# Walk products through three banks, row sums read out with their product, no transfers issued by GpSimd: a two-layer graph kernel on one core

## The chip, the core and the metric

The kernel runs on one core of a Trainium2 chip. The metric is the time of one execution in microseconds of device time. The kernel before took 1558.84 us, the median of three runs (1557.53 to 1560.49). Engines are named as the profile names them: PE is the matmul engine (TensorE), ACT is ScalarE, DVE is VectorE, POOL is GpSimd, and SP is the engine that only issues transfers.

## The reference

There are N = 2708 nodes with 256 features each, and a sparse adjacency matrix of N x N. Layer 0 does two steps, and each has a walk and an attention:

```python
R = S + jnp.eye(N); R = R / R.sum(-1, keepdims=True)     # S is adj
Xf, Xa, Z = X, X, 0
for n in range(2):
    A = top_p_attention(Xa, W1, W2, W3)   # softmax(q k^T), the largest entries up to a mass of 0.9, renormalised
    Xf = R @ Xf                            # the walk
    Xa = A @ Xa                            # the attention
    Z = Z + Xf @ U1[n].T + Xa @ U2[n].T
x = layernorm(X + layernorm(X + Z))
```

Layer 1 is a graph attention with four heads over the mask adj != 0 (with the diagonal set), a residual and a layer norm.

## The kernel before

**Tiles.** The nodes lie in 22 row tiles: 16 of 128 rows and 6 of 110, in 11 pairs (PAIRS). All data is fp32.

**The order of the work.** Each engine runs its instructions in the order in which the program issues them; only SP's transfers are put in order by the framework. The program hands out work in slots. `slot(spend)` advances the searches that are under way (`going`), then everything in `doing`, then one piece of the mixing, and then takes `spend` matmuls from the generator `walks()` (`stream`). A `yield` in one of these generators is thus a place where other work comes between.

**Attention.** For each tile, `search` makes the scores (L784 on PE, exponentials L788 on ACT), and in step 1 `survey` looks for a threshold: ACT goes over the row four times (`tally`, L809), and POOL works out the next threshold in between (L829 to L841, whose result is `rth`). DVE then cuts (`bound`, L857 to L878), finds maxima (L889), sorts (L902 to L918), and masks the row (L955, L958). `step` turns the masked row block by block (L259 on PE, the copy eT L264 on ACT) and multiplies it (L277 on PE) into the bank `att`, which ACT reads (L1286).

**The walk.** R @ X is done over pairs of tiles by a scheme of seven products in place of eight. `mixes()` builds the sums of adjacency blocks beside the first attention step (POOL, L720) and stores them as S1 to S4, D11 and D22. Each of the seven products of a pair takes one block as the stationary operand (11 pieces, loaded by SP three products ahead into four buffers, L670 and L682) and one operand from the node features or from their sums T1 to T4 (L1000 to L1006). A product is 11 matmul calls (L1086), which the profile counts as 22. Products lie in two banks, `walk0` and `walk1`, by turns. The order is D11, S2, A12, S3, S1, D22, S4 (PHASES). D11 and A12 accumulate in one bank, as do S2 and S3, and S1 and S4. When a product ends it is read out: ACT copies p1 (D11, L1093) and xa (A12, L1097); DVE makes y1 (S2, L1095), y2 (S3, L1099) and the rest of xa and xb (S1 L1101, D22 L1103, S4 L1105). In the first walk, A12 and S1 carry one column more, the row sums; DVE takes their reciprocal `rinv` straight from the bank (L1108).

After the first walk of a tile, `after_walk0` scales and adds on POOL (L1159, L1160) and stores the rows to `xmd` (L1161). Before the second walk the rows are fetched back (`return_rows`) and the sums T1 to T4 are made anew (`reblend`, `blend`); until that is done, the second walk may do only its first product. The second walk's results go to `finish` (ACT L1226, then POOL and norms), which makes the input of layer 1.

**When.** The first attention step runs without the walk. Then, between the steps, 14 walk calls go to a slot (SPEND_BETWEEN) while the first searches of step 1 begin. In step 1 each block of attention is followed by 11 or 12 walk calls (SPEND_1).

**Layer 1.** `neighbours` fetches a row of adjacency (L239) and makes it a mask with Sign and Square on ACT (L240, L241). `weights` makes the weights on DVE (L1566), `values` and `denominators` multiply them on PE (L1578, L1588). The first two masks are fetched and made at the third-last block of the last attention tile (`early`).

**Transfers that POOL issues.** Halves of q to the other partitions (L760), the terms c1, c2, c3 to DRAM (L1206, L1220, L1288), c1 back (`ca`, L1051), and the walk's rows (L1161).

Of the kernel before, what the change touches and what calls it, by code (L numbers as in the profile page):

```python
# [16 lines left out]
P = 128  # L17
# [28 lines left out]
def kernel(  # L46
# [186 lines left out]
    def neighbours(g, j, adjp):  # L233

        k = rows[j]
        i0, i1 = off[spans[g][0]], off[spans[g][-1] + 1]
        bar = adjp.tile([P, NT - HT, P], F32, name="blk")
        bar = bar.rearrange("p t d -> p (t d)")[:k, : i1 - i0]
        nc.sync.dma_start(bar, adjT[off[j] : off[j + 1], i0:i1])  # L239
        nc.scalar.activation(bar, bar, AF.Sign)  # L240
        nc.scalar.activation(bar, bar, AF.Square)  # L241
        if j in spans[g]:
            own = bar[:, off[j] - i0 : off[j + 1] - i0]
            nc.vector.tensor_tensor(own, own, ident[:k, :k], op=ALU.max)
        return bar
# [299 lines left out]
    def fast_layer0(ep, adjp):  # L545
# [196 lines left out]
        def project(s, c0, w, pj, xT, copy_q, copy_k):  # L742

            for lo, hi, h in ((c0, min(c0 + w, HN), 0), (max(c0, HN), c0 + w, 1)):
                if lo >= hi:
                    continue  # L750
                here, there = slice(h * DA, (h + 1) * DA), slice((1 - h) * DA, (2 - h) * DA)
                at = slice(lo - c0, hi - c0)
                for c in range(DC):
                    nc.tensor.matmul(
                        pj[:, at], wkqk[:, c, h : h + 2].rearrange("p h e -> p (h e)"),
                        xT[:, c, at], start=(c == 0), stop=(c == DC - 1),
                    )
                copy_k(kT[s][here, lo - h * HN : hi - h * HN], pj[here, at])
                copy_q(qT[there, lo:hi], pj[there, at])
                nc.gpsimd.dma_start(qT[here, lo:hi], qT[there, lo:hi])  # L760
# [233 lines left out]
        def blend(name, j0, j1, k):  # L994
# [22 lines left out]
        PHASES = (  # L1017
            ("D11", "B11", 0, True), ("S2", "T2", 1, True), ("A12", "B21", 0, False),
            ("S3", "T3", 1, False), ("S1", "T1", 0, True), ("D22", "T4", 1, True),
            ("S4", "B22", 0, False),  # L1020
        )

        def walks():
# [4 lines left out]
            queue = [(s, i, n) for s in range(STEPS) for i in range(PAIRS) for n in range(7)]  # L1028

            def load(s, i, n):  # L1030
                if (s * PAIRS * 7 + i * 7 + n) % 4 == 3:
                    blk = compact(fourth, rows[2 * i])
                else:
                    blk = new_block(rows[2 * i])
                key = PHASES[n][0]
                if key == "A12":
                    fetch(blk, 2 * i, 1)
                else:
                    get(key, i, blk)
                return blk  # L1040

            def beside(s, t):
# [7 lines left out]
                if not s:  # L1050
                    nc.gpsimd.dma_start(ca[:m], c1[t][:m])  # L1051
                    return ca, None
# [10 lines left out]
            blocks = [load(*queue[at]) for at in range(AHEAD)]  # L1063
            walking.append(True)
            yield
            for at, (s, i, n) in enumerate(queue):
                a, b = 2 * i, 2 * i + 1
                m = rows[a]
                _, name, bank, start = PHASES[n]
                while s and (owing & {(t, 0) for t in (NT - 2, NT - 1)} or (n and blending)):  # L1070
                    yield True
                blk = blocks.pop(0)
                if at + AHEAD < len(queue):
                    blocks.append(load(*queue[at + AHEAD]))
                if n == 0:
                    use = {}
                    xa, xb = (rowp.tile([P, D], F32, name="xw", bufs=4) for _ in range(2))
                if start:
                    use[bank] = ps_wk.tile([P, CHUNK], F32, name=f"walk{(bank + i) % 2}")
                if n == (3 if s else 0):  # L1080
                    aside = {t: beside(s, t) for t in (a, b)}
                w = HALF + 1 if s == 0 and n in (0, 2, 4) else HALF
                ac = use[bank][:m, :w]
                for j in range(PAIRS):
# [5 lines left out]
                    if j == PAIRS - 1:  # L1090
                        left = ac[:, :HALF]
                        if n == 0:
                            nc.scalar.copy(p1[:m], left)  # L1093
                        elif n == 1:
                            nc.vector.tensor_add(y1[:m], left, p1[:m])  # L1095
                        elif n == 2:
                            nc.scalar.copy(xa[:m, :HALF], left)  # L1097
                        elif n == 3:
                            nc.vector.tensor_add(y2[:m], left, p1[:m])  # L1099
                        elif n == 4:  # L1100
                            nc.vector.tensor_add(xb[:m, HALF:], left, y2[:m])  # L1101
                        elif n == 5:
                            nc.vector.tensor_add(xb[:m, :HALF], left, y2[:m])  # L1103
                        else:
                            nc.vector.tensor_add(xa[:m, HALF:], left, y1[:m])  # L1105
                        if s == 0 and n in (2, 4):
                            t = a if n == 2 else b
                            nc.vector.reciprocal(rinv[:m, t : t + 1], ac[:, HALF : HALF + 1])  # L1108
                        if (s, i) == (0, PAIRS - 1):
                            if n in (2, 4, 6):  # L1110
                                return_rows(n)
                            for t, xw, h in {
                                2: ((a, xa, 0),), 5: ((b, xb, 0),), 6: ((b, xb, 1), (a, xa, 1))
                            }.get(n, ()):
                                owing.add((t, h))
                                doing.append(last_rows(t, xw[:m], aside[t][0], h))
                                next(doing[-1])
                            if n == 6:
                                blending.append(True)
                                doing.append(reblend())  # L1120
                        else:
                            for t, xw, last in ((b, xb, 5), (a, xa, 6)):
                                if n == last:
                                    doing.append((after_walk0, finish)[s](t, xw[:m], *aside[t]))
                                    next(doing[-1])
                    yield
            walked.append(True)

        def return_rows(n):

            assert len(rows_kept) == NT - 2
            odd, cols = {2: (None, slice(0, HALF)), 4: (0, second), 6: (1, second)}[n]
# [22 lines left out]

        def after_walk0(t, xw, ca, _):
# [4 lines left out]
            nc.gpsimd.dma_start(xmd[:m, t], xw)  # L1161
# [30 lines left out]
        def terms1(t, xT):  # L1192
# [13 lines left out]
            nc.gpsimd.dma_start(c1[t][:m], cs[:m])  # L1206

        def terms2(t, xT):
# [11 lines left out]
            nc.gpsimd.dma_start(c2[t][:m], cs[:m])  # L1220
# [47 lines left out]
        def step(s, cur, spend):  # L1268
            turned_first = None
            for t in range(NT):  # L1270
# [11 lines left out]
                def between(n):  # L1282
                    last = n == len(groups) - 1
                    if last:
                        xa = heldp.tile([P, D], F32, name="xa1")
                        nc.scalar.activation(xa[:m], ac[:m, :D], AF.Copy, scale=rden)  # L1286
                        if s and t in c3:
                            nc.gpsimd.dma_start(c3[t][:m], xa[:m])  # L1288
# [5 lines left out]
                    if s and (t, n) == (NT - 1, len(groups) - 3):  # L1294

                        early.extend(neighbours(0, j, adjp) for j in first[:2])
# [468 lines left out]
```

## Time and profile before

| | |
|---|---|
| median of three runs | 1558.84 us |
| profiled execution | 1558.56 us, of which the span from the first to the last instruction is 1556.7 us |
| PE, mean granted clock | 0.989 |
| attention step 0 | about 70 to 441.9 us |
| between the steps | 441.9 to 524.9 us |
| attention step 1, with the rest of both walks | 524.9 to about 1200 us |
| layer 1 | from about 1200 us |
| transfers issued by POOL (software queue) | 14.58 MB, 2.9% of the DMA engines' span |
| HBM over the span | 162 GB/s |

The page gives the busy time of each engine, the same in 40 slices, the DMA queues, the chain that ended last and the costliest groups of instructions. A group's line has the source line, engine, operation, output and input, the count, the busy time with the mean of one, and the idle time before it with what ended it. The waits list has: who waited, for whom, us in total, how many times, the longest. A timeline line has start, duration, engine, line, operation and operands, and in brackets the idle time before it and what ended it.

### The profile page before, as it was taken

The numbers are of one execution on the slowest core, as the hardware profiler recorded it, in microseconds if no ns is written. First come the engines' busy times: TensorE is split into PE (matmuls) and PEld (weight loads), VectorE is DVE, ScalarE is ACT, GpSimd is POOL, SyncE is SP. The second block draws the span as 40 slices with busy tenths as digits, with TensorE's granted clock in tenths as the row PEclk, the third lists the DMA queues.
The fourth block names the chain that finished last, engine by engine and source line by source line (L and its number), as shares of the span: only waits on it lengthen the run. The fifth ranks groups of instructions, "written<-read, shape, count | busy, mean of one in ns | idle before, by whom it ended". The sixth has DMA issues, their size and how long they took to land. (4 is left out here: it accounts for less than half of the span.)

```text
span 1556.7 us, 29932 instructions
## 1 busy us (share of the span) xinstructions
PE 1496.2 (96%) x10537; PEld 1068.6 (69%) x10537; DVE 1295.4 (83%) x3763; ACT 801.1 (51%) x1472; POOL 642.4 (41%) x1063
## 2 busy tenths in 40 slices
PE   8999999999998899999989999999999999999993
PEld 4477777777787888888978888888887234333442
DVE  4599999999524887888889898989894998999994
ACT  3444444444334555655656666666653444556572
POOL 2267787865034223423443454544433300144142
PEclk9999999999998999999999999999999999999997
DMA  5198988894047555554555555654454365344331
GB/s 159 55 269 262 287 273 261 259 270 143 12 145 219 175 153 169 165 164 133 168 173 155 171 180 174 182 179 145 143 165 152 113 186 158 97 117 119 94 103 32
DMA packets 204210, 255.99 MB, mean 164 GB/s; under 512 B 42201, under 2 KB 166813, under 8 KB 204049
## 3 DMA queue, kind: packets, MB, share of 16 engines
q1 hardware_dynamic: 192224, 234.36, 50.0%
q0 software_dynamic: 5664, 14.58, 2.9%
q10 hardware_dynamic: 6161, 5.03, 1.1%
q8 instruction: 85, 1.39, 0.4%
q14 instruction: 76, 0.62, 0.1%
HBM read 190.10 MB, written 62.44 MB: 162 GB/s over the span
## 5 line engine op out<-in xcount | busy, mean ns | idle before, releaser
L809 ACT ACTIVATE junk<-e,minus,rth 128x2708 bf16<-128x2708 f32 (+1 forms) x88 | 232.9, 2647 | 60.0 <-POOL rth L841 59.2
L264 ACT COPY eT<-tr 128x512 f32<-128x512 f32 (+5 forms) x264 | 141.6, 536 | 214.0 <-PE tr L259 211.1
L277 PE MATMUL att<-xm,eT 128*128 128x256 f32 (+3 forms) x968 | 230.8, 379 | 0.3 <-ACT xa L1286 0.3
L277 PE MATMUL att<-ba,eT 128*128 128x256 f32 (+3 forms) x968 | 230.9, 379 | 0.0
L1578 PE MATMUL acc<-pt,v 128*32 128x512 f32 (+3 forms) x2112 | 221.2, 543 | 3.4 <-DVE pt L1566 2.3
L1566 DVE SCALAR_TENSOR_TENSOR pt<-e,tj,blk 128x1024 f32<-128x1024 f32 (+3 forms) x176 | 184.6, 1113 | 10.7 <-ACT blk L241 7.5
L1086 PE MATMUL walk<-xe,blk 128*128 128x128 f32 (+6 forms) x1452 | 180.8, 275 | 7.0 <-DVE xw L1105 2.4
L277 PEld LDWEIGHTS att<-xm,eT 128*128 128x128 f32 (+3 forms) x968 | 169.6, 186 | 22.0 <-ACT xa L1286 0.7
L277 PEld LDWEIGHTS att<-ba,eT 128*128 128x128 f32 (+3 forms) x968 | 169.5, 186 | 22.0 <-ACT eT L264 0.8
L1086 PEld LDWEIGHTS walk<-xe,blk 128*128 128x128 f32 (+3 forms) x1452 | 172.0, 187 | 17.2 <-issue 7.2
L788 ACT ACTIVATE e<-lg 128x1024 f32<-128x1024 f32 (+1 forms) x132 | 121.1, 922 | 108.5 <-PE lg L784 98.0
L1578 PEld LDWEIGHTS acc<-pt,v 128*32 128x32 f32 (+1 forms) x2112 | 73.3, 110 | 134.0 <-issue 99.5
L259 PE MATMUL tr<-ident,e 128*128 128x128 f32 (+3 forms) x968 | 147.5, 271 | 4.5 <-ACT eT L264 4.5
L1086 PE MATMUL walk<-xm,blk 128*128 128x128 f32 (+3 forms) x1100 | 140.9, 278 | 4.5 <-DVE xm L1002 2.8
L259 PEld LDWEIGHTS tr<-ident,e 128*128 128x128 f32 (+3 forms) x968 | 111.3, 139 | 46.7 <-issue 26.7
L1086 PEld LDWEIGHTS walk<-xm,blk 128*128 128x128 f32 (+3 forms) x1100 | 133.0, 189 | 14.4 <-issue 7.8
L1588 PE MATMUL acc<-pt,sb 128*32 128x512 f32 (+3 forms) x1056 | 114.8, 542 | 0.0
L1566 DVE SCALAR_TENSOR_TENSOR pt<-r,tj,blk 128x1024 f32<-128x1024 f32 (+1 forms) x88 | 109.8, 1311 | 1.3 <-issue 0.6
L240 ACT ACTIVATE blk<-blk 128x1024 f32<-128x1024 f32 (+3 forms) x66 | 63.3, 961 | 81.6 <-DMA blk<-in_adjT_dram 73.6
L889 DVE MAX8 cand<-e 128x8 f32<-128x170 f32 (+1 forms) x352 | 85.8, 320 | 22.1 <-ACT e L788 21.9
L889 DVE MAX8 cand<-scr 128x8 f32<-128x97 f32 (+1 forms) x616 | 102.8, 244 | 0.0
L907 DVE MAX8 top<-work 128x8 f32<-128x128 f32 (+3 forms) x242 | 82.3, 340 | 8.3
(271 smaller groups left out, 2448.1 us busy)
## 6 DMA issues: line engine op xcount, KB each, us to landing
blk<-in_adjT_dram SPq DMA_DIRECT2D x68, 512.0 KB
blk<-S SPq DMA_DIRECT2D x48, 512.0 KB
blk<-D SPq DMA_DIRECT2D x24, 512.0 KB
blk<-in_adjT_dram SPq DMA_DIRECT2D x26, 440.0 KB
D<-blk SPq DMA_DIRECT2D x16, 512.0 KB
S<-scr SPq DMA_DIRECT2D x16, 512.0 KB
S<-blk SPq DMA_DIRECT2D x16, 512.0 KB
xm<-S SPq DMA_DIRECT2D x16, 512.0 KB
```

The source lines that it names most:

```text
L240: nc.scalar.activation(bar, bar, AF.Sign)
L259: nc.tensor.transpose(tr[: rows[t], q, :m], e[:m, off[t] : off[t + 1]], ident[:m, :m])
L264: copy(eT[:k, : len(grp), :m], tr[:k, : len(grp), :m])
L277: nc.tensor.matmul(acc, eT[: rows[t], q, :m], value(t), start=(t == 0), stop=(t == NT - 1),)
L788: nc.scalar.activation(halves[:m, :, c0 : c0 + w], lg[:m, :, :w], AF.Exp, accum_out=zp[:m, n : n + 1],)
L809: nc.scalar.activation(junk[:m], e[:m], func, scale=rth, bias=minus1[:m], accum_out=acc)
L889: nc.vector.max(cand[:, n, :], src[:m, n * size : min(N, (n + 1) * size)])
L907: nc.vector.max(top[:, k : k + 8], work if k else flat)
L1086: nc.tensor.matmul(ac, blk[:k, j, :], MOVING[name](j, k, w), start=start and j == 0, stop=j == PAIRS - 1, skip_group_check=True,)
L1566: nc.vector.scalar_tensor_tensor(pt[:k, :gw], targets[g][h // 2][:k, h % 2, :gw], tj[:k, j, h : h + 1], bar, op0=ALU.max, op1=ALU.mult,)
L1578: nc.tensor.matmul(acc[h // 2][c][to : to + SIDE, :w], v[j][:k, h, o : o + SIDE], probs[n][h][:k, c0 : c0 + w], **at,)
L1588: nc.tensor.matmul(acc[2][c][h * SIDE : (h + 1) * SIDE, :w], sb[:k, j, h : h + 1].to_broadcast([k, SIDE]), probs[n][h][:k, c0 : c0 + w], **at,
```

## The change

- **Products.** They are named by number (1 D11, 2 A12, 3 S4, 4 D22, 5 S1, 6 S2, 7 S3), and their accumulations by X (1, 2), Y (6, 7), Z (5, 3) and W (4). There are three orders. TWO is the order of before. THREE, for the first three pairs of the first walk, goes 1, 6, 5, 2, 7, 3, 4 and turns through three banks, the third being `att`, which has no other use between the steps. FIRST, for the first pair of the second walk, goes 1, 2, 6, 5, 7, 3, 4, and the second walk may do two products, not one, before the sums T1 to T4 are there. A pair begins in the bank that the last product did not use.
- **Read-outs.** ACT now copies product 2 and product 5 with their row sums (129 columns); DVE takes the reciprocals from the copies. y2 is added to product 5 by POOL afterwards.
- **Transfers.** What POOL issued goes to SP or ACT. The store of the walk's rows comes a slot later than the sums.
- **Masks.** Each of the first two masks of layer 1 is fetched when a walk product ends, the fourth-last and the second-last, and made three slots later (`early_bar`).

```diff
     def neighbours(g, j, adjp):
+        parts = bars(g, j, adjp)
+        next(parts)
+        return next(parts)
+    def bars(g, j, adjp):
...
         nc.sync.dma_start(bar, adjT[off[j] : off[j + 1], i0:i1])
+        yield
         nc.scalar.activation(bar, bar, AF.Sign)
         nc.scalar.activation(bar, bar, AF.Square)
...
-        return bar
+        yield bar
...
-                nc.gpsimd.dma_start(qT[here, lo:hi], qT[there, lo:hi])
+                (nc.scalar if begun else nc.sync).dma_start(qT[here, lo:hi], qT[there, lo:hi])
...
-        PHASES = (
-            ("D11", "B11", 0, True), ("S2", "T2", 1, True), ("A12", "B21", 0, False),
-            ("S3", "T3", 1, False), ("S1", "T1", 0, True), ("D22", "T4", 1, True),
-            ("S4", "B22", 0, False),
-        )
+        PRODUCTS = {
+            1: ("D11", "B11", "X"), 2: ("A12", "B21", "X"), 6: ("S2", "T2", "Y"),
+            7: ("S3", "T3", "Y"), 5: ("S1", "T1", "Z"), 3: ("S4", "B22", "Z"), 4: ("D22", "T4", "W"),
+        }
+        THREE, TWO, FIRST = (1, 6, 5, 2, 7, 3, 4), (1, 6, 2, 7, 5, 4, 3), (1, 2, 6, 5, 7, 3, 4)
+        BETWEEN = 3
+        def order_of(s, i):
+            return THREE if s == 0 and i < BETWEEN else FIRST if (s, i) == (1, 0) else TWO
...
-                    nc.gpsimd.dma_start(ca[:m], c1[t][:m])
+                    nc.sync.dma_start(ca[:m], c1[t][:m])
...
-                while s and (owing & {(t, 0) for t in (NT - 2, NT - 1)} or (n and blending)):
+                while s and (
+                    owing & {(t, 0) for t in (NT - 2, NT - 1)} or (at % 7 > 1 and blending)
+                ):
                     yield True
...
+                    if order_of(s, i) is THREE:
+                        home = dict(zip("XYZW", ((7 * i + k) % 3 for k in (0, 1, 2, 6))))
+                    else:
+                        k = 1 if last_bank == 0 else 0
+                        home = dict(X=k, Y=1 - k, Z=k, W=1 - k)
...
+                start = chain not in use
                 if start:
-                    use[bank] = ps_wk.tile([P, CHUNK], F32, name=f"walk{(bank + i) % 2}")
+                    pool, label = (ps_wk, f"walk{home[chain]}") if home[chain] < 2 else (ps_at, "att")
+                    use[chain] = pool.tile([P, CHUNK], F32, name=label)
...
                         elif n == 2:
-                            nc.scalar.copy(xa[:m, :HALF], left)
+                            nc.scalar.copy(xa[:m, :w], ac)
-                        elif n == 4:
-                            nc.vector.tensor_add(xb[:m, HALF:], left, y2[:m])
+                        elif n == 5:
+                            nc.scalar.copy(xb[:m, HALF : HALF + w], ac)
...
-                        if s == 0 and n in (2, 4):
-                            t = a if n == 2 else b
-                            nc.vector.reciprocal(rinv[:m, t : t + 1], ac[:, HALF : HALF + 1])
+                        if s == 0 and n == 2:
+                            nc.vector.reciprocal(rinv[:m, a : a + 1], xa[:m, HALF : HALF + 1])
+                        if s == 0 and n == 5:
+                            nc.vector.reciprocal(rinv[:m, b : b + 1], xb[:m, D : D + 1])
+                        if n in (5, 7) and {5, 7} <= over:
+                            nc.gpsimd.tensor_add(xb[:m, HALF:D], xb[:m, HALF:D], y2[:m])
...
+                        if at in (len(queue) - 4, len(queue) - 2):
+                            doing.append(early_bar(first[0 if at == len(queue) - 4 else 1]))
+                            next(doing[-1])
...
+        def early_bar(j):
+            parts = bars(0, j, adjp)
+            next(parts)
+            yield
+            yield
+            yield
+            early.append(next(parts))
...
             nc.gpsimd.tensor_add(xw, xw, ca[:m])
-            nc.gpsimd.dma_start(xmd[:m, t], xw)
+            yield
+            nc.sync.dma_start(xmd[:m, t], xw)
...
-            nc.gpsimd.dma_start(c1[t][:m], cs[:m])
+            nc.sync.dma_start(c1[t][:m], cs[:m])
...
-            nc.gpsimd.dma_start(c2[t][:m], cs[:m])
+            nc.scalar.dma_start(c2[t][:m], cs[:m])
...
-                            nc.gpsimd.dma_start(c3[t][:m], xa[:m])
+                            nc.scalar.dma_start(c3[t][:m], xa[:m])
...
-                    if s and (t, n) == (NT - 1, len(groups) - 3):
-                        early.extend(neighbours(0, j, adjp) for j in first[:2])
```

## The prediction

> **What bounds the kernel now.** I read first the page's busy table and its slices, then TensorE's waits over the whole run, then the timelines of four engines round the waits found, then the clock there.
>
> ```profile
> PE 1496.2 (96%) x10537; PEld 1068.6 (69%) x10537; DVE 1295.4 (83%) x3763; ACT 801.1 (51%) x1472; POOL 642.4 (41%) x1063
> ```
>
> TensorE (PE) is busy for 96% of the span. So the change can save only part of 60.5 us of PE idle (1556.7 - 1496.2), and what PE loses at a lower clock. By stage (windows at 70, 441.9, 524.9, 1200.2, 1530) the idle is 7.4, 3.4, 9.1, 12.2, 4.7 and 23.7 us. The last is the tail, which the change leaves alone. The waits say whose it is:
>
> ```profile
> PE walk L1086 <- DVE rinv L1108: 5.5, 2, 3.8
> ...
> PE walk L1086 <- DVE xm L1002: 2.8, 1, 2.8
> PE walk L1086 <- DVE xw L1105: 2.4, 1, 2.4
> PE acc L1578 <- DVE pt L1566: 2.3, 1, 2.3
> ...
> PE walk L1086 <- DVE xw L1101: 1.8, 1, 1.8
> PE walk L1086 <- DVE u_sb L1095: 1.7, 1, 1.7
> ```
>
> Most are walk products that wait until the product two before has been read out of the bank that both use. The timeline of the longest one, on ACT, POOL, DVE and PE:
>
> ```profile
> 475.30 2.64 ACT L809 ACTIVATE junk<-e,minus,rth 128x2708 bf16<-128x2708 f32 x1 [7.08 <-POOL rth L841]
> 477.94 0.24 ACT L1097 COPY xw<-walk 128x128 f32<-128x128 f32 x1
> ```
> ```profile
> 468.44 0.70 POOL L1161 DMA_DIRECT2D xmd<-xw  x1 [0.30 <-POOL xw L1160]
> 469.14 1.09 POOL L1051 DMA_DIRECT2D ca<-c  x2
> ...
> 472.30 0.61 POOL L1161 DMA_DIRECT2D xmd<-xw  x1 [0.30 <-POOL xw L1160]
> ```
> ```profile
> 478.22 0.17 DVE L1108 RECIPROCAL rinv<-walk 128x1 f32<-128x1 f32 x1 [8.12 <-ACT xw L1097]
> ```
> ```profile
> 478.44 2.52 PE L1086 MATMUL walk<-xe,xm 128*128 128x129 f32 x10 [3.81 <-DVE rinv L1108]
> ```
>
> POOL issues DMAs before it makes the threshold (L841, at 475.08). ACT's third tally waits 7.08 us for that threshold. The copy of product A12 stands behind the tally, DVE's reciprocal from the same bank behind the copy, and PE behind the reciprocal. It then costs more than 3.81 us, as the windows show (columns: sum and count per engine, then the granted clock):
>
> ```profile
> 477.00:482.00 5.00, 3.56 (x14) 2.82 (x16) 1.51 (x10) 3.83 (x5) 0.00 (x0) 0.61 0.43 134
> 482.00:487.00 5.00, 5.00 (x28) 2.98 (x25) 4.32 (x12) 2.23 (x4) 0.19 (x1) 0.71 0.12 12
> ```
>
> Between the steps (441.9 to 524.9, 83.0 us) PE's work at full clock is 22.9 products of 2.456 us (22 matmuls from start to start) and 10.5 us of other matmuls (L784 three times 1.92 + 0.76, L754 0.70, L1213 1.71), together 66.7. So 16.3 us are lost: 9.1 idle, 7.2 slow.
>
> **What the Trainium skill says.** "TensorE: Matmul & The Clock Gate", Part 1: the clock falls to half after an idle window of about 3.4 us. The trace agrees: 0.61 and 0.71 after a gap of 3.81 us. "PSUM — Partial Sum Buffer", PSUM bank collisions: two engines must not touch one bank at once, not even to read. That is why L1108 waits for a copy of other columns of the same bank (8.12 us above). "DMA: Bandwidth & Descriptors", SWDGE vs HWDGE vs iDMA: GpSimd computes descriptors in software, SP's and ACT's are made in hardware. The trace agrees: a POOL issue is 0.54 to 0.65 us of POOL's time. "SBUF — State Buffer", on the port pair that VectorE and GpSimd share: who loses it blocks for the other's whole instruction. Here one L1167 took 3.32 us beside the 3.03 us L958, another 0.62.
>
> **The change, part by part.** All sums are against the profiled execution, 1558.56 us (span 1556.7 and 1.9 round it; the median of the runs is 1558.84). How the built kernel's instructions stand I take from the order of each queue.
>
> *Transfers off POOL.* 123 issues go (19 L760, 22 L1206, 22 L1220, 22 L1051, 20 L1161, 18 L1288), 72.5 us of POOL, which PE mostly doesn't see. They go to SP (7 qT, 22 c1 stores, 22 ca loads, 20 xmd stores) and ACT (12 qT, 22 c2, 18 c3).
> On SP, queued behind a waiting ca or xmd are the block loads. An xmd stands two slots after its product; the load after it must in any case wait for a product's buffer, which keeps about 7.3 us of lead (a load issued at 462.38 is used at 469.55). POOL needs 1.8 us a tile, so I take nothing; without that cover each xmd could cost 2 us. At the start the c1 stores stand ahead of the mixing's first loads, but those wait for POOL's memset at 77.78 anyway: nothing. The c1 stores do show on PE once: ACT's copy at 72.00 waits 2.20 us for a POOL store that took 3.8 us to land, and PE 1.96 us after it. The store of `shared` on SP released its reader in 2.6 us (1157.36 to 1159.94), which is soon enough: -1.5 (from -2 to +2, as four ca loads now wait on SP for stores to land).
> On ACT an issue lasts 0.35 us (L1554 on ACT's queue) and waits for the copy before it. Behind it stand the copies eT, for which PE leaves 1.7 us (one group of L277). So nearly all hides: 52 issues, +1.0 (0 to 4).
>
> *Between the steps.* Three banks give a read-out two products of cover, 4.9 us in place of 2.46. I walk the queues forward with the durations of the trace. POOL's chain loses 3.0 us of issues and gaps (0.70+1.09+0.61 and 2 x 0.30), so the threshold comes at 472.3, the third tally ends at 475.0, the copy of product 5 at 475.3, the fourth tally at 477.8. The next users of those banks come at 478.6 and 481.6: the 3.81 us are gone. **What is late next is DVE.** From 478.6 its queue is scalars 1.7, L874 3.0 and 0.4, read-out 0.2, maxima 2.3, two read-outs 0.4, maxima 2.4, sort 6.2: it reads y1 (product 6 of pair 2) at 495.2. PE, unhindered, wants that bank at 493.9 (441.9 + 18 x 2.456 + 7.8 of inserted matmuls): 1.5 us of wait. Then one of 1.6 (product 5's copy behind a third tally), one of 2.8 (product 3's read-out behind L958 and L874 of the next search: 512.2 against 509.5) and 0.4 in step 1: 6.3. The same walk of the queues of before gives 13.3 where the trace shows 16.3, since it has no slow clock; 6.3 x 16.3/13.3 = 7.7. Saved: 16.3 - 7.7 = **-8.6** (from -4, if DVE comes later still, to -14).
>
> *Product 5 by ACT, its sum with y2 by POOL; sums evicted.* L1101 goes from DVE, with its 1.85 us wait at 1155. ACT's two read-outs a pair made PE wait 0.44 us in all of step 1, so a third costs about 0.2. POOL gets 22 adds of 128x128: 0.46 each (L1170), up to 3.3 if it loses the port. The second walk's scaling on ACT (L1226) now waits for that add; I put 1.0 on this. Together -0.6 (from -1.9 to +2).
>
> *Opening of the second walk.* At 793.68 its first product waits 2.36 us because it takes the bank that the last one just left. Now it takes the other, read out at 784.9: -2.36. At 805.37 the third group waits 2.76 us for the blended sums (L1002), and 14 matmuls after it take 2.99 us instead of 1.73. With A12 second, S2 comes one product and one attention group later (2.5 + 2.2 us), while the chain that ends in L1002 starts with PE: it is ready 2 us before. -2.76 and -1.26. New: the second product follows the first on one bank and waits for ACT's copy, 0.27 and hand-over: +0.45. No tally stands before that copy. Sum **-5.9** (-3 to -6.5).
>
> *Masks.* ACT's queue holds the first mask's Sign and Square ahead of the last scalings, some 5 us earlier, so L1566 starts at about 1195 and not at 1200.80; PE's 2.31 us go. In their place eT copies come behind 2.1 us of mask work, twice about 0.3: **-1.7** (0 to -2.5).
>
> *What the lost pauses did.* DVE is busy 574 of 675 us in step 1 and used those pauses to catch up; I put +1.5 (0 to 4) for small waits in their place.
>
> Sum: -1.5+1.0-8.6-0.6-5.9-1.7+1.5 = -15.8; 1558.56 - 15.8 = 1542.8, and 0.3 to the median: **1543**.
>
> **Rivals.**
> *DVE paces it (0.20).* If DVE's queue is as late as before (-3 in place of -8.6 between the steps) and half of the 5.9 us comes back as waits: 1543 + 5.6 + 3.0 = about 1552. For: DVE has no gap from 508 to 530. Against: its own idle before that, 8.1 and 3.5 us for L1108, goes.
> *Starved of blocks (0.08).* The DMA engines are 97 and 98% busy from 467 to 477; a PE without pauses asks for 692 KB each 2.9 us, and xmd and ca add to it. With 7 us of waits: 1550. Against: at the 311 GB/s of that stretch a block takes 2.2 us.
> *Slower: ACT held by POOL's add (0.07).* In the second walk L1226 waits for an add that lost the port to DVE (3.3 us), and every eT copy queues behind. There are 11 such adds; at 2 us of PE each, 22 us: 1565. It decides from 1.4 us an add (15.8/11). Against: a slot of about 5 us lies between add and scaling.
> *All of it (0.05).* No wait is left between the steps, and the rest holds: 1535.
>
> **How the numbers follow.** Forecast 1543 (0.60, its own range 1538 to 1548). The range for 8 in 10 takes in the two rivals at 1550 and 1552 and most of the parts' low ends: 1536 to 1553. About 0.2%, 3.1 us, is what a measurement of this kernel can tell from no change. Slower: the ACT rival and a little of the others, 0.08. Same (over 1555.7): 0.07. Faster: 0.85.
>
> **What would show it.** PE's wait list without L1108, L1002, L1105 and pt; a clock near 1 between the steps; three walk waits there of 1.5 to 3 us, on DVE or ACT; the fourth tally's end at about 478; step 1 starting 8 to 9 us earlier; the same 2.456 us a product. Wrong if PE waits for DMA in the walks, if eT waits on ACT grow past 5 us in sum, or if DVE reads y1 of pair 2 as late as 501.

## The result, and the profile after

The changed kernel takes 1544.69 us (median of 6 runs, 1543.81 to 1548.63). The kernel before took 1559.47 in the same comparison (6 runs). The ratio is 0.9909, with a 95% interval from 0.9896 to 0.9922. The profiled execution took 1544.92 us, with a span of 1543.1 us.

That is 1.7 us from the 1543 that was forecast. But the gain does not lie where the forecast put it. To see this I took instructions that both kernels run in the same order (the copies eT, the exponentials, the weights pt), matched them by their number, and subtracted the start in the trace of before from the start in the trace of after:

| place | sum of the difference, us | this stage | forecast of the stage |
|---|---|---|---|
| first blocks of step 0 (105 us) | +0.2 | +0.2 | -1.5 |
| end of attention step 0 | +8.5 | +8.3 | +1.0 |
| first blocks of step 1 | -2.4 | -10.9 | -8.6 |
| end of the first walk | -2.8 | -0.5 | part of +1.5 |
| after the opening of the second walk (850 us) | -4.6 | -1.7 | -5.9 |
| before the last walk products (1150 us) | -4.3 | +0.3 | part of +1.5 |
| after product 5 of the last pair (1173 us) | -6.4 | -2.1 | -0.6 |
| layer 1 (from 1300 us on) | -6.6 | -0.2 | -1.7 |
| end of the span | -13.6 | -7.0 | 0 |

Busy times changed little:

```profile
PE 1494.1 (97%) x10537; PEld 1066.1 (69%) x10537; DVE 1275.3 (83%) x3741; ACT 807.7 (52%) x1494; POOL 590.6 (38%) x962
```

TensorE's waits over the whole run (who waited, for whom, us, times, longest):

```profile
PE tr L266 <- ACT eT L271: 11.9, 9, 3.3
...
PE walk L1109 <- DVE u_sb L1119: 2.7, 1, 2.7
...
PE walk L1109 <- DMA blk<-S: 1.4, 1, 1.4
...
PE acc L1614 <- DVE pt L1602: 1.2, 2, 0.6
...
PE walk L1109 <- DMA xm<-S: 0.9, 1, 0.9
```

The waits for L1108, L1002 and L1105 are gone, as they should be. The first line is new in size. In the trace of before the same wait reads:

```profile
PE tr L259 <- ACT eT L264: 4.5, 4, 2.0
```

The forecast had named three signs of being wrong. Two came: eT waits "past 5 us in sum", and PE waiting for DMA in the walks (the two lines with DMA, 1.4 and 0.9 us). The third did not: DVE reads y1 of the third pair at 494.6 us, once the later start of the walk is taken off (below).

**Attention step 0.** ACT's timeline at the first large gap:

```profile
112.09 0.37 ACT L766 COPY qT<-walk 64x256 f32<-64x256 f32 x1
117.64 0.50 ACTq L767 DMA_DIRECT2D qT<-qT  x1
118.18 0.59 ACT L271 COPY eT<-tr 128x512 f32<-128x512 f32 x1 [5.72 <-DMA scr<-in_adjT_dram]
```

PE's timeline at the same place, and the windows there (span, busy time and count of PE, PEld, DVE, ACT and POOL, then the clock, the DMA share and GB/s):

```profile
113.68 1.88 PE L1252 MATMUL walk<-u_sb,xT 128*128 128x512 f32 x4
118.82 1.10 PE L266 MATMUL tr<-ident,e 128*110 128x128 f32 x4 [3.25 <-ACT eT L271]
```
```profile
117.00:122.00 5.00, 3.18 (x10) 2.73 (x11) 4.93 (x7) 1.72 (x4) 5.00 (x6) 0.66 1.02 393
122.00:127.00 5.00, 5.00 (x26) 3.15 (x25) 3.88 (x5) 1.52 (x4) 5.00 (x3) 1.00 0.54 207
```

The half of q that ACT is to send is ready at 112.46, but ACT issues it at 117.64. What ended the wait is a load of an adjacency block for the mixing, which SP had issued. The copy eT stands behind the issue on ACT, and PE behind the copy: 3.25 us of gap, and then a clock of 0.66 over 5 us, which is 3.4 us at half clock. The queue of ACT in the built program says why (row, line, operation, what it waits for):

```
96 L767 DMACopy qT<-qT 64x256 [waits DMAHW0_49,Activation_49]
97 L271 TensorCopy eT<-tr 128x512 [waits PE_49]
100 L1259 DMACopy c_1_244<-cs 128x256 [waits DMAHW4_49,Activation_49]
```

All transfers of SP and ACT in this program take eight completion marks (DMAHW0 to 7) by turns, and an issue waits until the transfer that had its mark before has landed. The trace agrees: the 906 transfers of SP and ACT carry eight semaphores, each 113 or 114 times. Of ACT's 31 issues in step 0, 30 have their mark from a transfer of SP. Before seven of them ACT has nothing to do and waits, for 0.3 to 5.2 us, 12.6 in sum.

**Between the steps** the waits have shrunk further than the forecast said. ACT's timeline where the tally waited 7.08 us, and the windows there:

```profile
480.72 2.64 ACT L816 ACTIVATE junk<-e,minus,rth 128x2708 bf16<-128x2708 f32 x1 [3.94 <-POOL rth L848]
...
483.36 0.25 ACT L1125 COPY xw<-walk 128x129 f32<-128x129 f32 x1
```
```profile
475.00:485.00 10.00, 10.00 (x88) 9.63 (x88) 0.45 (x2) 6.05 (x7) 5.01 (x11) 1.00 0.89 272
485.00:495.00 10.00, 10.00 (x80) 8.44 (x77) 8.05 (x35) 5.09 (x11) 1.54 (x7) 1.00 0.85 266
```

PE is busy throughout, at full clock, while the tally and the copy behind it still end late. In the whole stage PE waits 1.45, 0.91 and 0.39 us, and 1.33 for the first copy eT of step 1. The first two are waits for blocks (at 504.92 and 508.52). SP's timeline ahead of the first:

```profile
500.10 0.33 SPq L1200 DMA_DIRECT2D xmd<-xw  x1
500.52 0.84 SPq L689 DMA_DIRECT2D blk<-S  x2
```

The load stands behind the store of the walk's rows, and that store waits for POOL's sum (L1198, done at 500.07). While it stands there the DMA engines are idle: 2% busy from 499 to 501 us.

The fourth tally (from 483.51, 2.64 us) ends at 486.15, which is 477.6 when one takes off the 8.6 us by which the walk begins later (forecast 478). DVE reads y1 of the third pair at 503.15, so 494.6 by the same reckoning (forecast 495.2).

**The opening of the second walk.** DVE's and then PE's timeline:

```profile
803.89 0.20 DVE L909 TENSOR_REDUCE fact<-cand 128x1 f32<-128x28 f32 x1
...
810.06 0.28 DVE L1119 TENSOR_TENSOR u_sb<-walk,u_sb 128x128 f32<-128x128 f32 x1
```
```profile
806.63 1.05 PE L1109 MATMUL walk<-xe,blk 128*128 128x128 f32 x8
810.40 2.35 PE L1109 MATMUL walk<-xm,blk 128*128 128x128 f32 x14 [2.71 <-DVE u_sb L1119]
```

Both old waits are gone. But product 7 adds onto the bank of product 6, so it waits until DVE has made y1 from it, and that addition stands behind a sort that begins at 803.89. The gap of 2.71 us is followed by 3.4 us at half clock, as were the 2.76 us before.

**The masks.** PE's gap of 2.31 us before the first weights has turned into one of 2.44 (ACT's Sign and Square, 1.06 us each, stand ahead of a copy eT) and two of 0.53 and 0.62.

**The end.** The last instruction with work starts at 1542.48 in before and at 1535.94 in after, so 6.5 us earlier, and yet the span is 13.6 us shorter. The difference is in what follows, and the view of the line to which the program's end is booked shows it, for before and for after (count, then ns of the shortest, the median and the longest):

```profile
L1761 POOLq DRAIN  x3: 40/106/10115, 1545.7 to 1556.4; - x3
```
```profile
L1797 POOLq DRAIN  x3: 34/50/223, 1536.6 to 1542.8; - x3
```

Before, POOL's drain at the end took 10.1 us, and the end came 0.83 us after it. After, it takes 0.05. (The other two drains of each line come later and take 0.03 to 0.22 us.) A drain is not counted as busy time, and the forecast left it out. It does not count in full: from the start of the last instruction with work to the end of the span are 14.2 us before and 7.2 after, so 7.0 of the 10.1 us show. The rest of the drain runs beside whatever fills those 7 us without it; which that is was not tested (the last rows' transfer is issued 0.6 us after that start).

### The profile page after: what moved, and what is told of

It is laid out like the page before. It is cut to its first block, busy times and chain, and to the rows that moved or that the text cites. A ratio compares the mean times of both kernels' runs of the same rounds, so it can differ in the third digit from the quotient of the medians.

```text
span 1543.1 us, 29894 instructions
## 1 busy us (share of the span) xinstructions
PE 1494.1 (97%) x10537; PEld 1066.1 (69%) x10537; DVE 1275.3 (83%) x3741; ACT 807.7 (52%) x1494; POOL 590.6 (38%) x962
## 3 DMA queue, kind: packets, MB, share of 16 engines
q8 instruction: 85, 1.39, 0.4%
## 5 line engine op out<-in xcount | busy, mean ns | idle before, releaser
L1109 PE MATMUL walk<-xe,blk 128*128 128x128 f32 (+3 forms) x1386 | 172.9, 275 | 1.2 <-ACT xw L1123 0.7
L1109 PEld LDWEIGHTS walk<-xe,blk 128*128 128x128 f32 (+1 forms) x1386 | 164.4, 187 | 11.4 <-issue 7.4
L1109 PE MATMUL walk<-xm,blk 128*128 128x128 f32 (+3 forms) x1034 | 130.4, 276 | 4.5 <-DVE u_sb L1119 2.7
L1109 PEld LDWEIGHTS walk<-xm,blk 128*128 128x128 f32 (+3 forms) x1034 | 123.3, 187 | 12.8 <-issue 6.1
L802 POOL TENSOR_TENSOR fact<-zp 128x1 f32<-128x1 f32 (+1 forms) x44 | 30.0, 681 | 170.2 <-ACT e L795 170.2
```

The lines of the kernel that those rows point to most:

```text
L802: nc.gpsimd.tensor_add(z, zp[:m, 0:1], zp[:m, 1:2])
L1109: nc.tensor.matmul(ac, blk[:k, j, :], MOVING[name](j, k, w), start=start and j == 0, stop=j == PAIRS - 1, skip_group_check=True,)
```

## The experiments

Stage times below are from the same matching of instructions against the trace of before. They come from one execution of each kernel. Where totals are compared, the runs of several rounds are.

**1. Which issues delay step 0: q and c2 back on POOL.**

```diff
-                (nc.scalar if begun else nc.sync).dma_start(qT[here, lo:hi], qT[there, lo:hi])
+                (nc.gpsimd if begun else nc.sync).dma_start(qT[here, lo:hi], qT[there, lo:hi])
...
-            nc.scalar.dma_start(c2[t][:m], cs[:m])
+            nc.gpsimd.dma_start(c2[t][:m], cs[:m])
```

> The changed kernel with the q halves (after the start) and the c2 stores issued by POOL again, as before the change; all else as changed. My theory: in attention step 0 an ACT-issued transfer waits until an older one of SP's has landed, and the copies eT stand behind it; so here the 8.4 us that step 0 lost come back, and the first walk product starts at about 442 us in place of 450.5. And as POOL issues software transfers again, its final drain takes about 10 us in place of 0.05 and the end comes 7 us later: 1544.7 - 8.4 + 7.0 = 1543.3. Rival A (step 0 is longer for another reason, such as ACT's or SP's own time): the first walk product stays at 450, 1551.7. Rival B (the short drain comes from elsewhere): 1536.3.

Measured: 1536.23 us (ratio to before 0.9852, 0.9836 to 0.9868). Step 0 loses nothing (0.0 from 77 to 431 us), the first walk product starts at 440.9 and not at 450.5, and between the steps the gain stays 10.9. ACT's issues were the cause. The drain took 2.85 us, neither 10 nor 0.05, so both the theory and rival B are wrong on its length:

```profile
L1797 POOLq DRAIN  x3: 40/107/2847, 1531.6 to 1535.0; - x3
```

But the total is rival B's. From the start of the last instruction with work to the end are 6.9 us, no more than the 7.2 of after: nothing of a drain of 2.85 us shows.

**2. The same transfers on SP.** Here both lines say `nc.sync`.

> The changed kernel with the same q halves and c2 stores on SP in place of ACT; POOL issues nothing. My theory: ACT waits for no landing any more, step 0 ends at about 442, POOL's drain stays short: 1544.7 - 8.4 = 1536.3. Rival A (ACT was not the cause): 1544.7. Rival C (on SP the q halves come too late behind the mixing's transfers, and the searches with them; the mixing's stores wait behind c2 stores): PE waits for q or for its cut rows in step 0, above 1541.

Measured: 1534.34 us (0.9841, 0.9824 to 0.9857). Step 0 loses 0.0 us here too, and PE's longest wait for eT is 1.0 us. SP waits 34.8 us in sum for c2 copies, with the mixing's transfers behind it, and nobody on the path minds. ACT's timeline at the old place now runs on without the issue:

```profile
112.25 0.37 ACT L766 COPY qT<-walk 64x256 f32<-64x256 f32 x1
112.64 0.59 ACT L271 COPY eT<-tr 128x512 f32<-128x512 f32 x1
```

**3. Only q moved to SP, c2 left on ACT.**

```diff
-                (nc.scalar if begun else nc.sync).dma_start(qT[here, lo:hi], qT[there, lo:hi])
+                nc.sync.dma_start(qT[here, lo:hi], qT[there, lo:hi])
```

> The changed kernel with only the q halves moved from ACT to SP; the 22 c2 stores stay on ACT. Theory: any issue on ACT waits for an older transfer to land, but the q halves waited longest (5.2 us at 112.5 to 117.6, and with it the slow clock); the c2 stores' own waits remain (2.3 us at most): step 0 loses 1 to 3 us in place of 8.4, so 1536.5 to 1538.5. Rival (q alone was the cause): as with both on SP, 1534.3. Rival (c2 was the cause): 1543 or more.

Measured: 1546.98 us (0.9928, 0.9913 to 0.9943), and step 0 loses 10.8 us. My theory named the wrong transfer: I had taken q for the worst, because the longest wait stood before it. In the trace of this kernel the next issue on ACT takes the wait over:

```profile
115.62 0.37 ACT L1257 COPY cs<-walk 128x256 f32<-128x256 f32 x1 [2.53 <-PE walk L1252]
...
120.41 0.35 ACTq L1259 DMA_DIRECT2D c<-cs  x1
120.80 0.58 ACT L271 COPY eT<-tr 110x512 f32<-110x512 f32 x1 [4.53 <-DMA D<-blk]
```

So the c2 stores alone are enough. That q alone would also be enough was not tried.

**4. What sets the drain: one transfer by POOL, and 66.** The first is the changed kernel with one store of c1 on POOL:

```diff
-            nc.sync.dma_start(c1[t][:m], cs[:m])
+            (nc.gpsimd if t == 0 else nc.sync).dma_start(c1[t][:m], cs[:m])
```

> The changed kernel with one single transfer issued by POOL, the first c1 store at about 30 us. My theory: any use of POOL's software queue makes its last drain long, however early: drain 10 us, 1544.7 + 7.0 = 1551.7, and nothing else changes. Rival (the drain is long by the number of transfers, or by recent ones): drain under 1 us, 1544.7. Rival (the drain varies from run to run): either, without order.

Measured: 1545.03 us (0.9912, 0.9895 to 0.9928), drain 0.144 us. "Any use" is wrong. The second is the kernel of experiment 2 with

```diff
-            nc.sync.dma_start(c1[t][:m], cs[:m])
+            for r0, r1 in ((0, 43), (43, 86), (86, m)):
+                nc.gpsimd.dma_start(c1[t][r0:r1], cs[r0:r1])
```

> The kernel with q halves and c2 stores on SP, and the 22 c1 stores at the start issued by POOL in three pieces of rows each: 66 software transfers with 2708 rows in all. POOL's final drain took 0.05, 0.14, 2.85 and 10.1 us with 0, 1, 34 and 123 software transfers. If it goes by their number: 0.05 + 66 x 0.082 = 5.5 us. If by their rows (0.72 ns each by the kernel before): 2.0 us. If by how late they were: 0.1 us.

```profile
L1798 POOLq DRAIN  x3: 34/107/5455, 1529.5 to 1535.6; - x3
```

The drain took 5.455 us, where the number of transfers gave 5.5 and their rows 2.0, and all 66 were issued in the first 80 us. With 0, 1, 34, 66 and 123 software transfers (those that POOL issues) it took 0.05, 0.144, 2.85, 5.46 and 10.1 us: 0.05 us and 0.082 us for each.

What this costs is less. From the start of the last instruction with work to the end, the traces have 6.5 to 7.2 us without software transfers, 7.1 with one, 6.9 with 34, 9.3 with 66 and 14.2 with 123. The total of the second kernel was 1538.61 us (median of only two runs; 0.9871, 0.9853 to 0.9889), 4.3 over experiment 2. Of these the end explains 2.8 (9.3 against 6.6); where the rest comes from stays open.

**5. The moves without the rest.** The kernel before, with its transfers issued as in after.

```diff
-                nc.gpsimd.dma_start(qT[here, lo:hi], qT[there, lo:hi])
+                (nc.scalar if begun else nc.sync).dma_start(qT[here, lo:hi], qT[there, lo:hi])
...
-            nc.gpsimd.dma_start(xmd[:m, t], xw)
+            yield
+            nc.sync.dma_start(xmd[:m, t], xw)
```

(c1, c2, c3 and ca alike.)

> The kernel before with the transfers moved off POOL as in the change, nothing else of it. My theory: step 0 is 8.4 us longer, the tail 7.0 shorter, and between the steps the third tally's threshold comes 2 to 3 us earlier, which shortens the wait of 3.8 us and spares one stretch of slow clock: -3 to -6 there. Sum 1559.5 + 8.4 - 7.0 - 4.5 = 1556.4 (1554.9 to 1557.9). If the three banks do all of the gain between the steps: 1561. If the transfers do all of it (-10.9): 1550.

Measured: 1550.99 us (0.995, 0.9933 to 0.9967), below what I expected. Step 0 +7.6, between the steps -9.4, end -7: the moves alone do most of what I had given to the banks. Its timelines where before had 3.81 us, of ACT and PE:

```profile
479.37 2.65 ACT L809 ACTIVATE junk<-e,minus,rth 128x2708 bf16<-128x2708 f32 x1 [3.95 <-POOL rth L841]
...
482.01 0.24 ACT L1097 COPY xw<-walk 128x128 f32<-128x128 f32 x1
```
```profile
482.51 1.38 PE L1086 MATMUL walk<-xe,xm 128*128 128x129 f32 x10 [0.65 <-DVE rinv L1108]
```

The tally's wait for the threshold is 3.95 us in place of 7.08, so PE's gap is 0.65 in place of 3.81, and the clock does not fall anywhere in this stage.

**6. The rest without the moves.** The changed kernel with all these transfers on POOL.

> The changed kernel with every transfer that the change moved issued by POOL again (the walk's rows right after their sums, as before): the change without the moves. With the moves alone 9.4 us went between the steps, with the whole change 10.9. Theory 1 (the moves and the three banks do the same work twice: either makes the late threshold harmless): between the steps -7 to -9 here too; with step 0 and start as before, the opening -1.8, product 5's wait of 1.85 gone, and the drain of 10 us back: 1559.0 - 8 - 1.8 - 2 = 1547. Theory 2 (the gain between the steps needs the moves, the banks add 1.5): 1559.0 - 1.5 - 1.8 - 2 = 1553.7. In both the fourth tally ends where it did before (about 481 us).

Measured: 1551.78 us (0.9951, 0.9935 to 0.9966). Between the steps -4.6, step 0 0.0, opening -1.8, drain 10.1 us. Neither theory: the value is between them. The third bank hides the late threshold in the first search: the tally there waits 7.10 us, and no walk product waits for the copy behind it. In the second it does not; the timelines of ACT and PE:

```profile
502.49 2.64 ACT L816 ACTIVATE junk<-e,minus,rth 128x2708 bf16<-128x2708 f32 x1 [7.20 <-POOL rth L848]
...
505.13 0.25 ACT L1125 COPY xw<-walk 128x129 f32<-128x129 f32 x1
```
```profile
505.43 0.49 PE L1109 MATMUL walk<-xe,xm 128*128 128x128 f32 x2 [3.69 <-ACT xw L1125]
```

So between the steps: moves alone 9.4, banks and read-outs alone 4.6, both 10.9. They overlap by 3.1.

**7. Two banks only.** Experiment 2 with `BETWEEN = 0` in place of 3.

> The kernel with q halves and c2 stores on SP, with the order of before (two banks by turns) also for the first three pairs; the row sums are still read out with their products, and the opening is the new one. Moves alone gave 9.4 of the 10.9 us between the steps. Theory: what the third bank adds there is 1.5 us or less: 1534.3 to 1535.8. Rival (the 1.5 us came from the read-outs of the sums, not from the bank): 1534.3. Rival (the third bank is what keeps PE from waiting): 1537 or more, as my prediction had it.

Measured: 1537.1 us (0.9865, 0.985 to 0.988; runs from 1534.91 to 1537.4). The interval just overlaps that of experiment 2 (0.985 against 0.9857), so the total doesn't settle it. In the trace the stage between the steps gains 10.0 us with two banks and 11.0 with three. But that trace is of the fastest of the four runs, and that of experiment 2 of the slowest of its four. The median lies where the last rival had it (1537 or more). What the third bank is worth beside the moves stays open: 1 us by the traces, 2.8 by the medians.

**8. The old place of the masks.** Experiment 2 with the call before's `early.extend(...)` and without `early_bar`.

> The kernel with q halves and c2 stores on SP, with the first two masks fetched and made where they were before (at the third-last block of the last attention tile). By my prediction of the masks' part: 1.7 us slower, 1536.0, with the wait of 2.31 us for the first weights back. My theory after the trace (ACT's mask work took that wait's place as waits of 1.01, 0.53 and 0.62 us): about the same, within 0.5 us of 1534.3. Rival: the old place is better now, 1533.

Measured: 1533.9 us (0.9848, 0.9833 to 0.9863) against 1534.34 in experiment 2: no difference that these runs can tell. In the traces, from the last walk products to layer 1, the old place moves the difference to before by +0.1 (with 3.4 us at half clock in it), the new one by -1.0 in experiment 2 and -0.2 in after.

**9. The addition behind the sort.** Experiment 2, with

```diff
+                        elif n == 6 and (s, i) == (1, 0):
+                            nc.scalar.copy(y1[:m], left)
                         elif n == 6:
                             nc.vector.tensor_add(y1[:m], left, p1[:m])
...
+                        if n == 7 and (s, i) == (1, 0):
+                            nc.gpsimd.tensor_add(y1[:m], y1[:m], p1[:m])
```

> The kernel with the q halves and c2 stores on SP (1534.3), and in the first pair of the second walk ACT copies product 6 out of its bank, POOL adds p1 one product later; DVE did both in one addition. Theory: product 7 waited 2.95 us for DVE's addition, which stood behind a sort, and 6.8 us of half clock followed (3.4 us lost); both go: 1534.3 - 2.95 - 3.4 = 1528.0. Rival (ACT's copy of product 5 behind the third tally, or DVE's next read-out, takes its place as the last to come): half of it, 1531. Rival (POOL's addition delays the threshold, and so that tally): 1534 or more.

Measured: 1533.78 us (0.984, 0.9826 to 0.9853). The wait of 2.95 us is gone. The first rival is right in kind: a read-out of DVE later in the same pair, behind the cut of the next search, is the next to be late. But its 1531 was not reached: the median is 0.6 us under experiment 2, which these runs cannot tell from nothing. DVE's and PE's timelines:

```profile
812.17 3.04 DVE L881 SCALAR_TENSOR_TENSOR scr<-e,hi 128x2708 f32<-128x2708 f32 x1
...
815.53 0.29 DVE L1131 TENSOR_TENSOR xw<-walk,u_sb 128x128 f32<-128x128 f32 x1
```
```profile
815.87 3.64 PE L1109 MATMUL walk<-xe,blk 128*128 128x128 f32 x16 [1.87 <-DVE xw L1131]
```

**10. The same edit for the third pair of the first walk** (`in ((0, 2), (1, 0))` in both lines).

> The kernel with q halves and c2 stores on SP and ACT's copy of product 6 in the first pair of the second walk (1533.8), with the same edit also in the third pair of the first walk, where product 7 still waits 1.7 us for DVE's addition behind a sort. Theory: ACT's copy lies between its second and third tally and comes 3 us before that addition did; the 1.7 us go: 1532.1. Rival (POOL's additions, two in a row there, delay the next search's threshold, or DVE's later read-outs take the wait over): 1533.8 or more.

Measured: 1533.25 us (0.9841, 0.9828 to 0.9855). The wait in that place stays, 1.66 us, now put down to the load of the block. Two things had been about equally late, and taking one away shows the other. By the median the total is 0.5 us lower, again less than these runs can tell.

**11. The walk's rows a slot later.** Experiment 10, with one more `yield` ahead of the store of xmd for the first six tiles.

> The kernel with q halves and c2 stores on SP and ACT's copies of product 6 (1533.3), and the stores of the walk's rows one slot later for the first three pairs. In that kernel PE waits 1.66 and 0.59 us between the steps for blocks whose loads stand on SP behind a store that waits for POOL's sum (load issued at 490.90, block used at 495.44). Theory: those loads start earlier, PE's two waits go, and nothing else is late in that place: between the steps -2.2, 1531.1. Rival (the loads wait for a buffer or for the DMA engines anyway): the waits stay, 1533.3. Rival (the stores stand ahead of other loads then): waits elsewhere, 1533.3 or more.

Measured: 1534.64 us (0.9839, 0.9826 to 0.9853; runs from 1531.89 to 1535.39). SP's order is the framework's, and it moved only one of the two stores: the block's load still stands behind a store, and its wait stays (1.64 us). The other load no longer does, and its wait of 0.59 us is gone; a DVE read-out behind it grew from 0.77 to 1.39. That speaks for the theory on SP, but the total shows nothing.

The versions of experiments 2, 9, 10 and 11 all lie at a ratio of 0.984, and their intervals end below 0.9896, where that of the changed kernel begins. So experiment 2, which moves two lines to another queue, beats both kernels by what these runs can tell; what the later edits add (0.6 and 0.5 us by the medians) is less than they can.

## Why the prediction was right in sum and wrong in its terms

**Transfers off POOL, the start: right.** In after and in the kernels of experiments 1, 2, 3 and 5 the loss between the exponentials at 26 us and the first blocks at 77 us is 1.1 to 1.2 us smaller (forecast 1.5). In after 1.4 us more were lost ahead of that, in the first loads, which differ between the traces of the other kernels by 0.0 to +1.5.

**Transfers on SP: a term at nothing that was not.** For block loads behind a waiting store the forecast had "so I take nothing; without that cover each xmd could cost 2 us". PE waited 1.45 and 0.91 us for two such loads. That the store ahead of them is the cause is read from SP's queue and not shown. Experiment 11 was to show it, but there the first load still stood behind its store and still came late; only the second load lost both, its store and its wait.

**Transfers on ACT: the step that failed.** "So nearly all hides: 52 issues, +1.0 (0 to 4)" became +8.3. The 0.35 us of an issue was right; 18 of the 52 (c3) stand in step 1 and cost nothing visible there. What I left out is the wait inside an issue. The order of the queues, which I had read, names the mark that each issue waits for; I priced the copy before it and not the mark. Experiments 1 and 2 show that the loss goes with the issuing engine, and experiment 3 that the c2 stores alone will do it.

**The tail: the second step that failed.** "The last is the tail, which the change leaves alone" missed 7.0 us. Of the 23.7 us that I called the tail, 10.1 were POOL's drain, at 0.082 us for each of 123 software transfers (experiment 4), and 7.0 of those stood alone.

**Between the steps: right in kind, -10.9 for -8.6.** The threshold came 3.2 us earlier against the walk's beginning (forecast 475.08 less 472.3, so 2.8), the order of events was as walked by hand, and DVE did not pace it. The term of the sum that was off is the scaling: I multiplied the 6.3 us of waits by 16.3/13.3 for the slow clock. But the slow clock is no share of the waits; with all gaps under 1.5 us it did not fall at all. The "7.2 slow" of before was a remainder, too: the clock's record has 10.2 us at half clock there, which loses 5.1. The 6.3 us itself was 4.7 (71.4 us of stage less 66.7 of work), and its longest wait was for a block and not for DVE. I also gave too much of the gain to the third bank, as experiments 5 and 6 show.

**Product 5: -2.1 for -0.6.** The wait of 1.85 us went, and neither POOL's additions nor ACT's third read-out took it back: the additions took 0.46 us in the median, two 3.1, and ACT's scaling (L1265) never waited for one.

**Opening: -1.7 for -5.9.** That the chain which ends in L1002 "is ready 2 us before" held, with 0.4 us. The sum stopped there, and did not ask when product 6 would be read out: its addition came behind a sort. The slow clock that was to go (-1.26) came back with it. Experiment 9 takes that wait away, and DVE is late again one product on, for 1.87 us with 3.4 us at half clock behind it. In its trace the opening gains about 3 us; but so does that of experiment 8, which kept the wait and where the clock did not fall.

**Masks: -0.2 for -1.7.** The mask work moved ahead of copies on the same engine and cost there what it had saved.

**Lost pauses: -0.2 for +1.5.** Nothing of the kind came.

The four largest errors are +7.3 (ACT), -7.0 (drain), +4.2 (opening) and -2.3 (between the steps). They cancel to +2.2. The mechanisms of the walk were read well, and the forecast was near, but two of its terms of 7 us were unseen, and that they had opposite signs was luck.

Of the rivals, "DVE paces it" and "ACT held by POOL's add" didn't come. Of "Starved of blocks", PE did wait for blocks, 2.4 us of its 7, but the first of these loads stood behind a store on SP while the DMA engines were 2% busy.

## What to carry to other kernels

When a transfer moves to another engine, price its wait as well as its issue: read from the built queue what the issue waits for, and what stands behind it. In this program ACT, which feeds TensorE, was a bad place for it while SP kept many transfers in flight. And a tail that no engine's busy time fills is not empty: look at the last line's instructions before you call it fixed.

## What was not expected of the hardware

- POOL's drain at the end takes 0.05 us and 0.082 us for each software transfer of the whole run, by their number and not their rows, and also for those that were issued in the first 80 us. With 34 of them no cost shows, with 66 about 2.8 us, with 123 about 7.
- What makes the clock fall is not the length of a gap alone. The gap at the opening was 2.71 us in after, 2.95 in experiment 2 and 2.90 in experiment 8. After it the records show 3.4 us at half clock, 6.8, and none. In each trace with several slow stretches, their starts lie a whole number of 3.413 us apart (in after 118.62 and 811.53, 203 of them). The Trainium skill ("TensorE: Matmul & The Clock Gate", Part 1) calls the activity window free-running, and this agrees: it depends on where a gap falls in the window.

  So I laid windows of 3.413 us over each trace, in step with its slow stretches, and added up PE's idle time in each (13 traces, from 70 to 1515 us; that of experiment 11 has no slow stretch). Of the windows that began at full clock, all 21 with more than 1.8 us idle were followed by half clock, none of the 5434 with less than 1.7, and two of the eight between. About half a window is thus enough, where the page speaks of an idle window of about 3.4 us. This case shows it by counting alone; no experiment moved a gap on purpose.

  In experiment 8 the edge of a window (at 799.68) cut the gap into 1.2 and 1.7 us; in experiment 2 2.30 us of it fell into one window. PE's lines after the gap, and the windows there, in experiment 2:

```profile
802.41 3.36 PE L1109 MATMUL walk<-xm,blk 128*128 128x128 f32 x14 [2.95 <-DVE u_sb L1119]
```
```profile
802.00:807.00 5.00, 4.59 (x20) 4.50 (x21) 4.69 (x23) 1.97 (x4) 0.00 (x0) 0.50 0.17 62
```

and in experiment 8:

```profile
801.37 1.83 PE L1109 MATMUL walk<-xm,blk 128*128 128x128 f32 x14 [2.90 <-DVE u_sb L1119]
```
```profile
802.00:807.00 5.00, 5.00 (x40) 4.80 (x39) 4.76 (x21) 3.81 (x6) 0.00 (x0) 1.00 0.02 4
```

The same 5 us hold 20 matmuls in one and 40 in the other.
